# A group-norm attention block with five engines in one written order: bias load behind x, stores and divisions a burst later, last pair's q and k ahead of the output projection

## The chip, the cores and the metric

The kernel runs on one core of a Trainium2 chip. The metric is the device time of one execution in microseconds (us), the median of several executions. A core has five engines that matter here: TensorE (PE, matrix products), VectorE (DVE), ScalarE (ACT), GpSimd (POOL) and SyncE (SP), which here only issues DMA transfers. Each engine takes its own instructions in order and waits, where it must, on semaphores that the others and the DMA queues raise.

## The reference, cut to what matters

```python
x: (4, 512, 48, 48) float32            # batch, channels, 2304 pixels
hn  = group_norm(x, 32 groups)         # over 16 channels x 2304 pixels each
qkv = einsum('oc,bchw->bohw', qkv_w, hn) + qkv_b      # 1536 x 512, to float16
w   = softmax((q * s)^T (k * s))       # 8 heads of 64 channels, 2304 x 2304
a   = einsum('bhts,bhcs->bhct', w, v)  # float32 again
out = x + einsum('oc,bchw->bohw', proj_w, a) + proj_b
```

## The kernel before, in words

**Tiles.** A batch is four chunks of 128 channels by 2304 pixels, held in blocks of 512 pixels, the last of 256 (`QBLOCKS`, j = 0 to 4). Two heads make a pair; there are 16 pairs (`NG`), four to a batch. For a pair and a block of 512 query pixels the kernel goes over the 18 tiles of 128 key pixels. Three such tiles make a **burst**: six matmuls for the scores of both heads (line 871), three exponentials of 128x1024 on ScalarE (line 878), and two bursts later (`BEHIND`) six matmuls with v (line 896). The list `stream` holds all bursts, 27 to a pair and 432 in all; block j = 4 has bursts of twice as many matmuls of half the width. The row sums of the softmax are kept by VectorE, which adds each burst's exponentials into `acc` (line 929, two folds in line 932), and by a matmul with ones over the result (`add_up`, line 949).

**Filler.** All other matrix work is cut into pieces that stand in one list, `beside`: projections to q and k of later pairs (`pqk`, line 696), to v (`pv`, line 741), and the output projection of the batch before (`pr`, line 798). `fill(n)` runs once per burst n and issues as many pieces as a credit allows, in the order of the list; a piece may have an earliest burst and a condition. If the head of the list isn't allowed yet, the burst goes without filler. `do_tasks`, called at the start of `fill`, issues the small work of the next batch's normalisation: `bn_stats` (line 605), and 20 normalisations in place (line 647) on VectorE. The v projection of the next batch has a condition: its blocks must have been issued for normalisation.

**After a block of queries.** `values` copies the result out of PSUM (`avx`, line 905). `rows` in `add_up` copies the sums (`slx`, line 959) and sends them by DMA into a narrow tile (line 963). A burst later `check_sums` tests their range on POOL (lines 986 and 987) and `invert` takes the reciprocal and writes it to DRAM (lines 993 and 995). Another burst later `divide` loads it back, spread over 64 partitions per head (`ib`, line 1005), and multiplies on POOL (`att`, line 1008). `direct` blocks, the last two of the last pair, are divided on VectorE without the way through DRAM.

**Output projection.** `att32` casts four `att` tiles to a wide type (line 792, on POOL) into `a32`, of which there is one buffer; `proj_chain` makes eight matmuls per 128 output channels; `proj_end` adds bias and residual (line 809, VectorE) and stores at once (line 812). The residual is loaded two chunks ahead (line 770) into a tag `res` of three buffers, which the store must have left. `chain_bank` gives one PSUM bank (`pw`) to all filler.

**Start.** x of batch 0 and the weights are loaded, statistics are taken chunk by chunk of 128 channels, ScalarE normalises (line 654), and six q and k chains run over the chunks in an outer loop `for c`. Between the chains stand two small matmuls with `gmat` for the group mean (line 622, after chain i = 1) and the variance (line 631, after chain i = 3) of the next chunk. `gmat` is made on POOL by a memset and two selections (line 565). The bias of v reaches all partitions through a DRAM row `brow` and a broadcast `bv` (lines 522 and 526), both issued by POOL.

**Order.** The program is traced in one order. PE and DVE keep that order; the instructions of the other three engines are ordered by a scheduler:

```python
    with tc.manual_schedule(engines={mybir.EngineType.PE, mybir.EngineType.DVE}):
        fast_path(tc, flag, *args)
```

`general_path`, behind a test at the end, isn't run with this data.

Of the kernel before, what the change touches and what calls it, by code (L numbers as in the profile page):

```python
# [26 lines left out]
P = 128  # L27
# [440 lines left out]
def fast_path(  # L468
# [37 lines left out]
    def load_block(b, j):  # L506
# [13 lines left out]
    bv = const.tile([P, C], F32, name="bv")  # L520
    brow = dram.tile([1, C], F32, tag="brow", bufs=1, name="brow")
    nc.gpsimd.dma_start(
        brow.rearrange("a (n p) -> a n p", p=P),
        qkv_b[:, 2 * NC :].rearrange("p n -> n p").unsqueeze(0),
    )
    nc.gpsimd.dma_start(bv, brow.to_broadcast((P, C)))

# [14 lines left out]
    load_w(2, slice(0, C), nc.sync)  # L542

# [214 lines left out]

    atts, res, at32 = {}, {}, {}

    def residual(b, j, m):
        o, n = QBLOCKS[j]
        if at_end(b, j):

            tag = f"x{m}_{j - NQ + 2}"
            xt = xpool.tile([P, QB], F32, tag=tag, name=f"r_{b}_{j}_{m}")[:, :n]
        else:
            xt = work.tile([P, QB], F32, tag="res", bufs=3, name=f"r_{b}_{j}_{m}")
            xt = xt[:, :n]
        nc.sync.dma_start(xt, x[b, bass.ts(m, P), o : o + n])  # L770
        res[b, j, m] = xt
# [34 lines left out]
    def proj_end(b, j, m, ps):  # L806
        o, n = QBLOCKS[j]
        xt = res.pop((b, j, m))
        nc.vector.scalar_tensor_tensor(  # L809
            xt, ps[:, :n], bproj[:, m : m + 1], xt, ALU.add, ALU.add  # L810
        )
        nc.sync.dma_start(out[b, bass.ts(m, P), o : o + n], xt)

    def proj_pieces(b, j):


        n = QBLOCKS[j][1]

        def run(chunk):
            bank = chain_bank(f"pr_{b}_{j}_{chunk[0]}")  # L820
            places = [bank[:, i * n : (i + 1) * n] for i in range(len(chunk))]
            for m, ps in zip(chunk, places):
                proj_chain(b, j, m, ps)
            for m, ps in zip(chunk, places):
                proj_end(b, j, m, ps)

        def ahead(k):
            if k < NQ * NC and not at_end(b, k // NC):
                residual(b, k // NC, k % NC)

        convert = [
            piece(0.0, lambda: att32(b, j, (NC - 1,) if at_end(b, j) else range(NC)))
        ]
        chains = []
        per = QB // n
        for m in range(0, NC, per):
            chunk = range(m, m + per)
            loads = [j * NC + i + 2 for i in chunk]
            if (j, m) == (0, 0):
                loads = [0, 1] + loads  # L840
            chains.append(
                [piece(0.0, lambda i=i: ahead(i)) for i in loads]
                + [piece(QB / 290.0, lambda chunk=chunk: run(chunk), True, True)]
            )
        return convert, chains
# [3 lines left out]
    av, acc, pts, avx, sums, rowd = {}, {}, {}, {}, {}, {}  # L849
# [61 lines left out]
    def add(u):  # L911
# [6 lines left out]
        if last and direct(g, j):  # L918
            acc[g, j].append(pt)
            return  # L920
# [14 lines left out]
    def add_up(g, j):  # L935
# [31 lines left out]
        if direct(g, j):  # L967
            source = rows() if n == QB else sl
            inv = work.tile([P, QB], F32, tag="rows", name=f"inv_{g}_{j}")
            nc.vector.reciprocal(inv[:, :n], source[:, :n])  # L970
            nc.vector.tensor_tensor(
                atts[g][:, o : o + n], avx.pop((g, j))[:, :n], inv[:, :n], ALU.mult
            )
            if source is sl:
                rows()
        else:
            rows()
# [22 lines left out]
    def divide(g, j):  # L1000
        o, n = QBLOCKS[j]
        row = rowd.pop((g, j))
        ib = work.tile([P, QB], F32, tag="rows", name=f"ib_{g}_{j}")
        for h in range(2):
            nc.sync.dma_start(
                ib[h * D : (h + 1) * D, :n], row[h : h + 1, :n].to_broadcast((D, n))
            )
        nc.gpsimd.tensor_tensor(  # L1008
            atts[g][:, o : o + n], avx.pop((g, j))[:, :n], ib[:, :n], ALU.mult
# [13 lines left out]

    now = [0]
    tasks, loads = deque(), deque()
    normed, turn = set(), {}
# [24 lines left out]
    def group_scale(b):  # L1053
        group_rstd(b, norm_bank(b))
        tasks.append((now[0] + 1, lambda: coefficients(b)))
        for j in range(NQ):
            for c in range(NC):

                def run(j=j, c=c):
                    norm(b, j, c)  # L1060
                    normed.add((b, j, c))
# [16 lines left out]
    def put_v(b, half):  # L1078
        for i in range(0, NT, 2):
# [3 lines left out]
            if half == 0:  # L1083
                pieces[0][4] = lambda last=last: last in normed
# [5 lines left out]
    def ready(b, j):  # L1090

        return BEHIND + (2 if direct((b + 1) * NPAIR - 1, j) else 5)
# [11 lines left out]
    for b in range(B):  # L1104
# [13 lines left out]
        if b == B - 1:  # L1118
            put_convert(old, 0)
            put_qk(g + 3, 1)  # L1120
            for j in range(NQ):
                put_qk(g + 3, 0, (j,))
# [3 lines left out]
            for j in range(NQ - 2):  # L1126
                put_convert(b, j)
                put_proj(b, j)
                if j < 2:
                    for m in range(NC):  # L1130
                        put_run(residual, b, NQ - 2 + j, m)
# [59 lines left out]
    for c in range(NC):  # L1191
# [4 lines left out]
        for i, chain in enumerate(chains):  # L1196
            chain(c)
            if c + 1 < NC and i == 1:
                group_mean(0, small_bank(f"mean_0_{c + 1}"), (c + 1,))
            if c + 1 < NC and i == 3:  # L1200
# [16 lines left out]
    def fill(n):  # L1217
# [6 lines left out]
        do_tasks(5 if idle else 0 if ended(n - 1) else 1 if ended(n - BEHIND - 1) else 2)  # L1224
# [28 lines left out]
    for n in range(end):  # L1253
# [16 lines left out]
        if ended(n - BEHIND - 3):  # L1270
            divide(*stream[n - BEHIND - 3][:2])
# [8 lines left out]
    att32(B - 1, NQ - 1, (NC - 1,))  # L1280
    while beside:
        issue()
    check_sums(NG - 1, NQ - 1)
    for pieces in projs[B - 1, NQ - 1][1]:
        for p in pieces:
            p[1]()
# [10 lines left out]
def group_norm_attention(ctx: ExitStack, tc: tile.TileContext, *args):  # L1297
# [3 lines left out]
    with tc.manual_schedule(engines={mybir.EngineType.PE, mybir.EngineType.DVE}):  # L1301
# [46 lines left out]
```

## Time and profile before

| | |
|---|---|
| time, median of three runs | 1676.22 us (1675.67 to 1679.45) |
| span of the profiled execution | 1674.1 us |
| PE busy | 1597.4 us (95%) |
| DVE busy | 1131.2 us (68%) |
| ACT busy | 1246.4 us (74%) |
| POOL busy | 363.0 us (22%) |
| one exponential of 128x1024 (L878) | 1028 ns mean, 1296 of them |
| one add into `acc` (L929) | 1804 ns mean |
| one cast for the output projection (L792) | 904 ns mean |
| one division (L1008) | 1596 ns mean |
| one residual or output transfer of 256 KB | 2.8 and 2.4 us from issue to landing |

The page gives for each engine its busy time and share of the span; for groups of instructions their line, engine, operation, output and inputs, count, busy time, mean duration, and the idle time of the engine ahead of them with what ended it. "Issue" is idle time in which nothing in the profile was waited for. Windows can be asked for separately: each gives the busy time of every engine in a stretch of the span, the number of instructions, and the granted share of the TensorE clock (PEclk).

### The profile page before, as it was taken

What the parts mean: (1) busy time and instruction counts of PE and PEld (TensorE: products, weight loads), DVE (VectorE), ACT (ScalarE), POOL (GpSimd) and SP (SyncE); (2) the same over time, 40 slices, a digit from 0 to 9 for tenths busy, and PEclk for the clock granted to TensorE, in tenths of its full rate; (3) what the DMA queues carried; (4) which work ended last, traced back from release to release, by engine and by line L of the source; (5) the groups of instructions that cost most, each with busy time, mean ns of one, the idle gap of its engine ahead of it and who ended that gap; (6) DMA issues with size and microseconds to landing.
All of it is one profiled execution on the core that took longest, in us unless ns stands there. A gap on an engine that the chain in (4) does not pass through costs nothing.

```text
span 1674.1 us, 28357 instructions
## 1 busy us (share of the span) xinstructions
PE 1597.4 (95%) x11516; PEld 699.1 (42%) x11516; DVE 1131.2 (68%) x1284; ACT 1246.4 (74%) x1317; POOL 363.0 (22%) x500
## 2 busy tenths in 40 slices
PE   3999999989999999989999999999999999999897
PEld 1443344334333443545433344345533334444445
DVE  3247666887666667867666766787766666676774
ACT  2158788867887878867777878777777888877982
POOL 1002221211121111232112111233232122233431
PEclk9999999999999999999999999999999999999999
DMA  8001001300000003440200000353010000044232
GB/s 213 1 8 33 14 12 47 97 14 11 14 17 14 15 11 89 118 130 21 45 14 18 14 11 14 93 147 103 11 48 17 14 14 11 14 111 120 74 100 92
DMA packets 94908, 82.11 MB, mean 49 GB/s; under 512 B 50928, under 2 KB 61040, under 8 KB 94768
## 3 DMA queue, kind: packets, MB, share of 16 engines
q1 hardware_dynamic: 93168, 78.87, 17.7%
q8 instruction: 92, 1.51, 0.4%
q10 hardware_dynamic: 1344, 1.05, 0.2%
q0 software_dynamic: 256, 0.28, 0.1%
q14 instruction: 48, 0.39, 0.1%
HBM read 60.70 MB, written 19.17 MB: 48 GB/s over the span
## 4 chain that ended last, share of the span: by engine, by line
PE 89%; DVE 3%; ACT 3%; DMA 2%; POOL 1%; issue 1%; SPq 0%; POOLq 0%; DVEq 0%; ACTq 0%
PE pqk L696 29%; PE ps L871 18%; PE av L896 17%; PE pv L741 15%; PE pr L798 8%; ACT p L878 3%; PE sl L949 1%; PE ps L696 1%; DVE acc L929 1%; DMA brow<-qkv_b_dram 1%; POOL a L792 1%; DMA ib<-row 1%; DMA out_dram<-r 0%; DVE r L809 0%; POOL att L1008 0%
## 5 line engine op out<-in xcount | busy, mean ns | idle before, releaser
L878 ACT ACTIVATE p<-ps 128x1024 f16<-128x1024 f32 x1296 | 1231.5, 1028 | 363.3 <-PE ps L871 363.3
L929 DVE TENSOR_TENSOR acc<-acc,p 128x3072 f16<-128x3072 f16 x270 | 487.0, 1804 | 65.5 <-ACT p L878 65.2
L696 PE MATMUL pqk<-x,wqkv 128*64 128x512 f32 (+1 forms) x2464 | 518.2, 551 | 2.5 <-DVE r L809 1.7
L871 PE MATMUL ps<-q,k 64*128 64x512 f16 (+1 forms) x2880 | 363.9, 359 | 16.0 <-ACT p L878 14.7
L896 PE MATMUL av<-p,v 128*64 128x512 f16 (+1 forms) x2880 | 361.7, 365 | 0.0
L741 PE MATMUL pv<-wqkv,x 128*64 128x256 f32 x2304 | 269.4, 380 | 5.2 <-DVE x L647 5.0
L986 POOL TENSOR_SCALAR in<-sums 128x8 f32<-128x8 f32 (+1 forms) x160 | 111.5, 697 | 727.6 <-DMA sums<-slx 719.8
L696 PEld LDWEIGHTS pqk<-x,wqkv 128*64 128x64 f32 x2464 | 168.8, 137 | 229.1 <-issue 171.8
L871 PEld LDWEIGHTS <-k 64*128 64x128 f16 x2880 | 107.7, 94 | 296.5 <-issue 250.3
L896 PEld LDWEIGHTS <-v 128*64 128x64 f16 x2880 | 131.9, 109 | 210.5 <-issue 166.6
L1008 POOL TENSOR_TENSOR att<-avx,ib 128x512 f16<-128x512 f32 (+1 forms) x78 | 124.5, 1596 | 418.9 <-DMA ib<-row 381.0
L741 PEld LDWEIGHTS pv<-wqkv,x 128*64 128x64 f32 x2304 | 159.7, 137 | 99.7 <-DVE x L647 9.0
L929 DVE TENSOR_TENSOR acc<-p,p 128x3072 f16<-128x3072 f16 x80 | 141.4, 1768 | 0.3 <-ACT p L878 0.3
L798 PE MATMUL pr<-a,whi 128*128 128x512 f32 (+1 forms) x320 | 125.2, 399 | 8.9 <-POOL a L792 8.0
L798 PE MATMUL pr<-a,wlo 128*128 128x512 f32 (+1 forms) x320 | 117.4, 375 | 0.0
L705 DVE TENSOR_SCALAR q<-pqk,bqkv 128x512 f16<-128x512 f32 (+1 forms) x79 | 54.9, 695 | 89.9 <-PE pqk L696 89.5
L932 DVE TENSOR_TENSOR acc<-acc 128x1024 f16<-128x1024 f16 x156 | 110.8, 711 | 5.3
L749 DVE TENSOR_TENSOR v<-pv,bv 128x512 f16<-128x512 f32 x72 | 49.7, 691 | 92.7 <-PE pv L741 92.1
L705 DVE TENSOR_SCALAR k<-pqk,bqkv 128x512 f16<-128x512 f32 (+1 forms) x75 | 52.2, 696 | 78.1 <-PE pqk L696 77.8
L905 DVE COPY avx<-av 128x512 f32<-128x512 f32 (+1 forms) x80 | 51.0, 638 | 69.1 <-PE av L896 69.0
L809 DVE SCALAR_TENSOR_TENSOR r<-pr,bproj,r 128x512 f32<-128x512 f32 (+1 forms) x80 | 55.2, 695 | 62.2 <-PE pr L798 56.8
L792 POOL CAST a<-att 128x512 fp32r<-128x512 f16 (+1 forms) x78 | 68.1, 904 | 94.5 <-PE pr L798 93.7
(62 smaller groups left out, 457.5 us busy)
## 6 DMA issues: line engine op xcount, KB each, us to landing
r<-x_dram SPq DMA_DIRECT2D x64, 256.0 KB, 2.8
out_dram<-r SPq DMA_DIRECT2D x64, 256.0 KB, 2.4
ib<-row SPq DMA_DIRECT2D x126, 128.0 KB, 3.0
x<-x_dram SPq DMA_DIRECT2D x62, 256.0 KB, 3.1
x<-x_dram SPq DMA_DIRECT2D x16, 128.0 KB, 2.4
sums<-slx SPq DMA_DIRECT2D x128, 2.0 KB, 2.1
r<-x_dram SPq DMA_DIRECT2D x16, 128.0 KB, 2.2
out_dram<-r SPq DMA_DIRECT2D x16, 128.0 KB, 1.8
```

Of the source, the lines that this page charges most:

```text
L696: nc.tensor.matmul(pw[0][lo : lo + D, :n], wqkv[:, c, w0 + lo : w0 + lo + D], hn[b, c, j], start=(c == 0), stop=(c == NC - 1),)
L705: nc.vector.tensor_scalar(qk[g][part][:, o : o + n], pw[0][:, :n], bqkv[:, col : col + 1], SCALE, ALU.add, ALU.mult,)
L741: nc.tensor.matmul(pw[0][lo : lo + D, a, :], hn[b, c, i * P // QB][:, at + lo : at + lo + D], wqkv[:, c, 2 * C + half * C // 2 :][:, : C / ...
L792: engine.tensor_copy(at32[b, j][c], atts[b * NPAIR + c][:, o : o + n])
L798: nc.tensor.matmul(ps[:, :n], w[:, c, bass.ts(m, P)], at32[b, j][c], start=(c == 0 and i == 0), stop=(c == NC - 1 and i == 1),)
L871: nc.tensor.matmul(ps[:, h, a * n : (a + 1) * n], kt[rows, bass.ts(i, P)], qt[rows, o : o + n], start=True, stop=True,)
L878: nc.scalar.activation(pt[:, r], ps, AF.Exp)
L896: nc.tensor.matmul(av[0][lo : lo + D, :n], vv[b, pr // 2][:, i, pr % 2 * P + lo : pr % 2 * P + lo + D], pt[:, r, h, a * n : (a + 1) * n], ...
L929: nc.vector.tensor_tensor(t, before, pt, ALU.add)
L932: nc.vector.tensor_tensor(t[:, 0], t[:, 0], t[:, r], ALU.add)
L986: nc.gpsimd.tensor_scalar(t, sm, limit, None, op)
L1008: nc.gpsimd.tensor_tensor(atts[g][:, o : o + n], avx.pop((g, j))[:, :n], ib[:, :n], ALU.mult)
```

## The change

All five engines now follow the traced order, so POOL, SP and ACT wait exactly where the program puts their instructions. The author's purpose is to place loads, stores and divisions so that no queue stands still for something late. With it come these edits:

- **Bias load**: `brow` and `bv` go from POOL's queue, ahead of `gmat`, to SP's queue, behind x and the weights.
- **Start loop**: group mean after chain i = 0 instead of 1, variance after i = 2 instead of 3.
- **Stores and residuals**: a store is issued one burst after its addition; a residual is loaded one chunk ahead instead of two; the 256-wide blocks move two chunks by one transfer instead of two.
- **Divisions**: `divide` is split into `spread` (the loads of `ib`) and the multiplication one burst later, except in the last pair.
- **Normalisation**: `do_tasks` gets 2 or 4 tasks per burst where the filler stands still, instead of 5; a v piece waits until its blocks were normalised in an earlier burst.
- **Output projection**: conversion allowed six bursts after the sums instead of five; in the last batch q and k of the last pair come ahead of the output projection of batch 2, where they were mixed.
- **End**: the very last block sums three tiles by matmul instead of adding on VectorE first, and the second to last block's division moves from VectorE to POOL.

```diff
-    nc.gpsimd.dma_start(bv, brow.to_broadcast((P, C)))
...
     load_w(2, slice(0, C), nc.sync)
+    bv = const.tile([P, C], F32, name="bv")
+    brow = dram.tile([1, C], F32, tag="brow", bufs=1, name="brow")
+    nc.sync.dma_start(
+        brow.rearrange("a (n p) -> a n p", p=P),
+        qkv_b[:, 2 * NC :].rearrange("p n -> n p").unsqueeze(0),
+    )
+    nc.sync.dma_start(bv, brow.to_broadcast((P, C)))
...
-                proj_end(b, j, m, ps)
+            xt = res.pop((b, j, chunks[0]))
+            for i, m in enumerate(chunks):
+                nc.vector.scalar_tensor_tensor(
+                    xt[:, i], places[i], bproj[:, m : m + 1], xt[:, i], ALU.add, ALU.add
+                )
+            loads.append(
+                (now[0] + 1, lambda: nc.sync.dma_start(rows_of(out, b, j, chunks), xt))
+            )
...
-        if last and direct(g, j):
+        if direct(g, j) and (last or j == NQ - 1):
             acc[g, j].append(pt)
...
-            nc.vector.tensor_tensor(
+            engine = nc.vector if source is sl else nc.gpsimd
+            engine.tensor_tensor(
                 atts[g][:, o : o + n], avx.pop((g, j))[:, :n], inv[:, :n], ALU.mult
             )
...
-                pieces[0][4] = lambda last=last: last in normed
+                pieces[0][4] = lambda last=last: normed.get(last, now[0]) < now[0]
...
-        return BEHIND + (2 if direct((b + 1) * NPAIR - 1, j) else 5)
+        if b < B - 1:
+            return BEHIND + 6
+        return BEHIND + (2 if j >= NQ - 2 else 5)
...
         if b == B - 1:
+            put_qk(g + 3, 1)
+            put_qk(g + 3, 0)
             put_convert(old, 0)
-            put_qk(g + 3, 1)
             for j in range(NQ):
-                put_qk(g + 3, 0, (j,))
                 put_proj(old, j)
...
-            if c + 1 < NC and i == 1:
+            if c + 1 < NC and i == 0:
                 group_mean(0, small_bank(f"mean_0_{c + 1}"), (c + 1,))
-            if c + 1 < NC and i == 3:
+            if c + 1 < NC and i == 2:
                 group_rstd(0, small_bank(f"var_0_{c + 1}"), (c + 1,))
...
-        do_tasks(5 if idle else 0 if ended(n - 1) else 1 if ended(n - BEHIND - 1) else 2)
+        do_tasks(
+            (2 if idle else 0)
+            if ended(n - 1)
+            else (2 if idle else 1) if ended(n - BEHIND - 1) else 4 if idle else 2
+        )
...
-        if ended(n - BEHIND - 3):
-            divide(*stream[n - BEHIND - 3][:2])
+        if ended(n - BEHIND - 3) and not direct(*stream[n - BEHIND - 3][:2]):
+            spread(*stream[n - BEHIND - 3][:2])
+            if n >= end - per_pair:
+                divide(*stream[n - BEHIND - 3][:2])
+        if ended(n - BEHIND - 4) and stream[n - BEHIND - 4][:2] in ibs:
+            divide(*stream[n - BEHIND - 4][:2])
...
-    with tc.manual_schedule(engines={mybir.EngineType.PE, mybir.EngineType.DVE}):
+    kinds = mybir.EngineType
+    engines = {kinds.PE, kinds.DVE, kinds.Pool, kinds.SP, kinds.Activation}
+    with tc.manual_schedule(engines=engines):
```

## The prediction

> **What bounds the kernel now.** I read the page's busy times first (PE 1597.4 of 1674.1 us: the bound, with 76.7 us idle), then windows, to see where the idle lies. Columns: window, length, then busy us and count per engine, TensorE clock, DMA share, GB/s.
>
> ```profile
> 18.00:30.00 12.00, 5.75 (x16) 2.57 (x18) 7.43 (x22) 3.42 (x5) 1.39 (x3) 1.00 0.98 325
> 30.00:60.00 30.00, 24.70 (x118) 8.28 (x116) 11.09 (x36) 10.25 (x15) 1.66 (x3) 1.00 0.18 65
> 60.00:300.00 240.00, 238.78 (x1800) 103.61 (x1798) 144.27 (x150) 164.85 (x174) 37.90 (x47) 1.00 0.10 24
> 320.00:370.00 50.00, 40.76 (x310) 17.33 (x308) 41.84 (x65) 36.34 (x40) 12.20 (x16) 0.93 0.10 27
> 700.00:770.00 70.00, 63.04 (x396) 32.17 (x396) 48.74 (x70) 44.79 (x48) 17.75 (x28) 0.95 0.36 108
> 810.00:830.00 20.00, 18.33 (x118) 7.02 (x116) 12.74 (x14) 13.98 (x15) 4.83 (x9) 1.00 0.36 87
> 1090.00:1170.00 80.00, 76.04 (x482) 39.38 (x480) 64.42 (x85) 58.03 (x62) 30.43 (x33) 1.00 0.42 124
> 1560.00:1600.00 40.00, 30.16 (x209) 12.93 (x207) 28.59 (x29) 37.41 (x41) 17.12 (x20) 1.00 0.25 54
> ```
>
> PE idles 18 us before the first window, 6.3 and 5.3 in the first two, then 1.2, 9.2, 7.0, 1.7, 4.0 and 9.8 us; between them (370 to 700, 830 to 1090, 1170 to 1560) it is never idle, so nothing can be won there. The waits of PE name the causes:
>
> ```profile
> PE mean L622 <- POOL gmat L565: 18.9, 1, 18.9
> PE ps L871 <- ACT p L878: 14.7, 33, 0.5
> PE pr L798 <- POOL a L792: 8.0, 5, 4.9
> PE sl L949 <- DVE avx L905: 6.8, 4, 2.7
> PE pv L741 <- DVE x L647: 5.0, 5, 1.7
> ```
>
> The timeline of the start tells why gmat is late: its second selection stands on POOL behind bv, which waits for brow.
>
> ```profile
> 3.67 1.15 POOL L522 DMA_DIRECT2D brow<-qkv_b_dram  x1
> 9.13 0.29 DVE L610 BATCH_NORM_AGGREGATE mv<-st 128x2 f32<-128x30 f32 x1
> 17.89 0.57 POOL L526 DMA_DIRECT2D bv<-brow  x1 [12.27 <-DMA brow<-qkv_b_dram]
> 18.48 0.34 POOL L565 TENSOR_SCALAR_AFFINE_SELECT gmat<-gmat 128x128 f32<-128x128 f32 x1
> 24.55 3.42 ACT L654 ACTIVATE x<-x,gb,ga 128x512 f32<-128x512 f32 x5 [19.07 <-DVE gb L642]
> ```
>
> The largest single gap later is the pr wait of 4.9 us at 714: POOL's division waits for ib, and SP had sat on stores and residual loads.
>
> ```profile
> 713.77 0.47 SPq L1005 DMA_DIRECT2D ib<-row  x1
> 717.22 1.26 POOL L1008 TENSOR_TENSOR att<-avx,ib 128x512 f16<-128x512 f32 x1 [4.55 <-DMA ib<-row]
> 718.42 1.72 POOL L792 CAST a<-att 128x512 fp32r<-128x512 f16 x3
> ```
>
> **What the Trainium skill says.** "PSUM — Partial Sum Buffer", section "Engine vs sequencer instructions": the queues of ScalarE, VectorE and GpSimd are strict FIFO. The trace agrees: a selection of 0.34 us waits 12.27 us behind a DMA issue. "DMA: Bandwidth & Descriptors", section "Rules for kernel authors": a strided last dimension "lowers to one descriptor per element". brow is such a transfer; its 2 KB took 13.9 us, and in the first 30 us the DMA answer shows 390 GB/s at best but 14 to 27 GB/s between 12.75 and 16.5 us, while x was still outstanding. "TensorE: Matmul & The Clock Gate", section "What's actually happening": half clock after an idle window of about 3.4 us. The trace agrees: after the 4.9 us gap the granted clock was 0.80 in 710 to 720 and 0.86 in 720 to 730. "SBUF — State Buffer", section "Who interferes with whom": VectorE and GpSimd lock a shared port pair. Four casts took 2.39 us at 697 and 3.81 at 1123, which fits.
>
> **The change part by part.**
>
> *Start.* Without bv ahead, gmat ends near 6 us, and the first mean can start once mv is there, 9.13 + 0.29 = 9.4 us instead of 18.88: 9.4 us won. From mean to the first normalisation took 24.55 - 18.88 = 5.7 us, of which 2.8 are statistics of chunk 1, so these are wanted at 11.5 us. x and the first weights are 5.2 MB; at about 370 GB/s from 3 us on they land by 17 us, chunk 1 by 12, chunk 3 by 17 (wanted at 23): not in the way. The cycle of one chunk was 6.7 us (33.45, 40.19, 46.92), 0.87 of it PE waiting for ScalarE, since the variance stood after chain 3; one chain earlier is 0.97 us earlier, which closes it, three times: 2.6 us. Sum 12.0. bv is needed by the first v at about 59 us; issued near 17 us it has 40 us for the 14 and 6 us that brow and bv took: free. Bounds 9 to 13.
>
> *First change of batch (320 to 370).* The compiled order has nine bursts without filler instead of six, since v waits a burst longer and normalisations come slower. VectorE bounds here. From the add of a block's last burst at 328.74 to the sums of the next block at 360.3 before took 31.6 us, with 7.5 us of v work inside (64 matmuls, 16 per 1.89 us), so 24.1 without. The new order of the same stretch on VectorE is six adds of 1.74, four folds of 0.76, 8 statistics (5.1 in all with the aggregates), 2 avx and 2 slx of 0.69, 5 normalisations of 0.63 and 1.5 us of small ones: about 26. So 1.9 us worse, plus up to 2 of its own waits; 1.5 us of waiting for x, which came after (361), goes. I take 2 worse, bounds 4 worse to 2 better.
>
> *Second (700 to 830).* Idle 7.0 + 1.7, and about 1.9 us of half clock under busy PE: 10.5. With ib issued a burst (3.6 us) before the multiplication and stores that SP no longer waits long for (the DMAs take 2.4 to 3.0 us), the 4.9 and 1.7 go. What stays: a32 has one buffer, so each of four changes of block may cost 0.7, as a gap at 1110 shows (casts 0.95 us each against 0.47 us of matmuls): 2.8. New: one burst without filler. Such a burst costs 0.84 (ten of them at 1560 to 1600 waited 8.4 us for ScalarE). With 0.5 for VectorE: 4.1, so 6.4 won, bounds 4 to 8.5.
>
> *Third (1090 to 1170).* Idle 4.0; after: the same 2.8 and one new burst without filler: 0.3 won.
>
> *Last batch.* Before, bursts 406 and 408 to 417 have no filler, eleven, and 9.8 us of idle. After, burst 408 and 415 to 417: four, 3.4 us. But pr of batch 2 is now in one run, where qk pieces gave POOL time: three changes of block of 0.7, and 0.6 for the sums: 6.1. Won 3.8, bounds 1.5 to 5.5. Divisions in the last pair wait for ib on POOL, but 8 us or more pass before their casts are needed.
>
> *Tail.* PE waited 2.71 us at 1646.8 for avx behind division (0.69) and add (1.75) on VectorE:
>
> ```profile
> 1646.08 0.69 DVE L971 TENSOR_TENSOR att<-avx,inv 128x512 f16<-128x512 f32 x1
> 1646.69 1.75 DVE L929 TENSOR_TENSOR acc<-p,p 128x3072 f16<-128x3072 f16 x1
> ```
>
> Both leave; twelve more ones matmuls (0.65 us for twelve) come: 1.6 won. Merged 256-wide transfers are off the path.
>
> Sum: 12.0 - 2.0 + 6.4 + 0.3 + 3.8 + 1.6 = 22.1 us, 1676.2 - 22.1 = 1654.1.
>
> **Waits added.** Every ib load now sits on SP behind a store that waits for VectorE's addition of the burst before; POOL's casts stand behind a multiplication that waits for ib. Both are a burst old when met, against 3 us of DMA: no wait in a burst of 3.6 us, a short one in a burst of 2.75.
>
> **Rivals.** (1) Start and tail only: DVE stalls and added bursts without filler (5 new ones, 7 gone) eat the middle: 1676.2 - 13.6 = 1662.6. For it: VectorE has 41.8 of 50 us in the first change. Against: the two POOL stalls are queue order, which is what changes. (2) More than forecast: casts hide (there was no gap over 0.3 us at the changes of block at 697 and 733), VectorE catches up: 2.8 + 2 + 3 more, 1646. (3) Slower: in strict order POOL or SP blocks for something the scheduler used to step around. One stall as at 714 costs 4.9 + 1.9 = 6.8 us; four such beyond those removed, with no gain in the middle: 1662.6 + 27 = 1690. Against: only x reloads, which wait for PE, and stores could do it, and neither stands before work that is due within a burst.
>
> **How the numbers follow.** Forecast 0.62, rival 1 0.23, rival 2 0.10, rival 3 0.05. The range reaches from rival 2 to past rival 1: 1645 to 1666. All but rival 3 are faster by over 0.2% (3.4 us); a tie would need half of rival 3's stalls: 0.02.
>
> **What would show it.** Mean L622 starting near 9.4 us and no bv on POOL; normalisation cycle near 5.9 us; PE idle about 11 us in the first change of batch; no pr wait over 2 us, and no half clock at the second; waits of pr for a summing to 8 us; ps for p about 13; sl for avx at the end under 1 us. Wrong would be: DVE or POOL waits over 3 us new in PE's list, x landing later than 20 us, or v waiting for bv.

## The result, and the profile after

The kernel after takes 1661.52 us (median, 1660.74 to 1665.11); the kernel before took 1676.01 us beside it. The ratio is 0.9913, 95% interval 0.9894 to 0.9932: 14.5 us less. The forecast was 22.1 us less (1654.1 us); the result is inside the range, and where the first rival put it (1662.6 us). Of the profiled executions the span fell from 1674.1 to 1659.0 us, and all of it is idle time of TensorE: PE is busy for 1597.6 us (1597.4 before) and idle for 61.4 us (76.7 before).

The windows of the kernel after, laid round the same stages as before (columns: window, length, busy us and count of PE, PEld, DVE, ACT, POOL, then TensorE clock, DMA share, GB/s):

```profile
0.00:15.50 15.50, 1.14 (x4) 1.00 (x4) 8.19 (x22) 2.02 (x3) 4.28 (x16) 1.00 0.94 304
15.50:60.00 44.50, 41.65 (x206) 15.59 (x208) 15.77 (x45) 12.94 (x20) 1.67 (x3) 1.00 0.32 96
310.00:350.00 40.00, 30.68 (x222) 12.37 (x222) 36.51 (x54) 33.66 (x37) 10.16 (x11) 0.96 0.22 54
670.00:760.00 90.00, 84.04 (x546) 44.15 (x542) 70.24 (x94) 63.35 (x68) 26.43 (x38) 0.98 0.43 125
1080.00:1160.00 80.00, 73.69 (x476) 38.69 (x474) 63.31 (x83) 54.98 (x59) 28.08 (x36) 1.00 0.40 119
1490.00:1560.00 70.00, 64.73 (x405) 32.59 (x402) 46.91 (x47) 51.37 (x55) 27.58 (x33) 1.00 0.41 120
1560.00:1600.00 40.00, 36.17 (x227) 17.78 (x226) 28.96 (x30) 33.21 (x36) 14.45 (x19) 1.00 0.43 130
1600.00:1659.00 59.00, 46.33 (x324) 30.13 (x321) 29.55 (x37) 23.77 (x26) 15.29 (x28) 0.95 0.37 123
```

Length less PE busy is the idle of each stage:

| stage | idle before, us | idle after, us | won | forecast |
|---|---|---|---|---|
| start, 0 to 60 | 29.5 | 17.2 | 12.3 | 12.0 |
| first change of batch | 9.2 | 9.3 | -0.1 | -2.0 |
| second change | 8.6 | 6.0 | 2.7 | 6.4 (with half clock) |
| third change | 4.0 | 6.3 | -2.4 | 0.3 |
| last batch, to 1600 | 9.8 | 9.1 | 0.7 | 3.8 |
| tail | 14.1 | 12.7 | 1.5 | 1.6 |

The start and the tail are as forecast. The middle, forecast at 8.5 us, brought 0.9 us of idle. Half clock adds a little: outside its last microseconds the kernel before has TensorE busy for 9.1 us at half clock and the kernel after for 6.1 us, so 1.5 us less are lost, 1.1 of them at the first change and 0.4 at the second. With it the first change came 1.0 us better and the second 3.1 us.

The waits of PE in the kernel after (what waited, for whom: us in total, times, longest):

```profile
PE ps L892 <- ACT p L899: 14.9, 33, 0.5
PE pr L819 <- POOL a L813: 10.8, 13, 1.5
PE mean L622 <- DVE mv L610: 9.1, 1, 9.1
PE sl L970 <- DVE avx L926: 4.7, 3, 2.1
PE pr L819 <- DVE r L839: 3.3, 3, 2.7
```

The wait for `gmat` is gone (the first mean now waits for `mv`), and so is the single wait of 4.9 us for a cast. In its place stand thirteen waits for casts, 10.8 us in all where there were five with 8.0, and a new one of 2.7 us for the residual addition `r`.

The start is as the steps had it. Its timeline (start us, length, engine, line, operation; in brackets the idle before it and its releaser):

```profile
4.00 0.76 POOL L565 TENSOR_SCALAR_AFFINE_SELECT gmat<-gmat 128x128 f32<-128x128 f32 x2
9.11 0.55 PE L622 MATMUL mean<-mv,gmat 128*128 128x1 f32 x2 [9.11 <-DVE mv L610]
14.76 3.42 ACT L654 ACTIVATE x<-x,gb,ga 128x512 f32<-128x512 f32 x5 [9.42 <-DVE gb L642]
32.31 0.35 SPq L542 DMA_DIRECT2D bv<-brow  x1
```

`gmat` ends at 4.8 us, the first mean starts at 9.1 us (9.4 forecast), the first normalisation at 14.8 us (24.6 before), and the later ones follow 5.9 us apart (23.67, 29.54, 35.42), as forecast. `bv` is issued at 32 us, lands at 38.2 us, and v first needs it at 60.1 us. x profits too: its last block lands at 17.8 us, where it landed at 27.2 us before. `brow`, a transfer of 2 KB, is no faster at its new place (15.4 to 32 us, and from 25 us on next to nothing else moves), but now nothing that is due stands behind it.

The new wait at the second change (the same columns):

```profile
674.62 1.05 SPq L791 DMA_DIRECT2D r<-x_dram  x2
676.07 2.98 SPq L503 DMA_DIRECT2D x<-x_dram  x4
680.50 0.75 DVE L839 SCALAR_TENSOR_TENSOR r<-pr,bproj,r 128x512 f32<-128x512 f32 x1 [4.32 <-DMA r<-x_dram]
681.31 0.80 PE L819 MATMUL pr<-a,whi 128*128 128x512 f32 x1 [2.69 <-DVE r L839]
```

The first residual is issued 2.5 us before its addition could start (the matmuls end at 677.1 us), and behind four x reloads, issued from 670.2 us on, that only land between 676 and 679 us. It lands 6 us after its issue; the addition waits, and PE behind it, since all filler has one PSUM bank. The matmul after the gap takes 0.80 us where the same one takes 0.50 elsewhere: half clock.

The kind of wait that is new at the third change:

```profile
1094.46 1.27 POOL L1034 TENSOR_TENSOR att<-avx,ib 128x512 f16<-128x512 f32 x1 [7.49 <-DVE st L605]
1095.68 4.73 POOL L813 CAST a<-att 128x512 fp32r<-128x512 f16 x4
1097.87 0.50 PE L819 MATMUL pr<-a,whi 128*128 128x512 f32 x1 [1.51 <-POOL a L813]
```

Four casts of an older block stand in GpSimd's queue behind a division of a newer one, and that waits for its `ib`, which SyncE issued at 1090.6 us after it had stood at a residual load that needed a store's buffer. (The row names a statistics instruction of VectorE that has nothing to do with `att`; the transfer of `ib`, which landed at 1094.3 us, is what the division needs. What `ib` is loaded from had itself landed only at 1089.7 us, so the stand at the residual cost 0.9 us at most.)

### The profile page after: what moved, and what is told of

Read it like the earlier page. It is cut to its first block, busy times and chain, and to the rows that moved or that the text cites. A ratio compares the mean times of both kernels' runs of the same rounds, so it can differ in the third digit from the quotient of the medians.

```text
span 1659.0 us, 28335 instructions
## 1 busy us (share of the span) xinstructions
PE 1597.6 (96%) x11528; PEld 699.7 (42%) x11528; DVE 1131.3 (68%) x1282; ACT 1246.5 (75%) x1317; POOL 370.8 (22%) x499
## 3 DMA queue, kind: packets, MB, share of 16 engines
q10 hardware_dynamic: 1344, 1.05, 0.2%
## 4 chain that ended last, share of the span: by engine, by line
PE 87%; DVE 4%; DMA 3%; POOL 3%; ACT 2%; issue 1%; SPq 0%; ACTq 0%; DVEq 0%; POOLq 0%
PE pqk L696 28%; PE ps L892 17%; PE av L917 17%; PE pv L741 15%; PE pr L819 7%; POOL a L813 2%; ACT p L899 2%; DVE acc L950 2%; PE ps L696 1%; PE sl L970 1%; DMA row<-inv 1%; DVE acc L953 1%; DMA ib<-row 1%; DMA out_dram<-r 1%; DVE st L605 0%
## 5 line engine op out<-in xcount | busy, mean ns | idle before, releaser
L892 PE MATMUL ps<-q,k 64*128 64x512 f16 (+1 forms) x2880 | 362.3, 358 | 17.0 <-ACT p L899 14.9
L1034 POOL TENSOR_TENSOR att<-avx,ib 128x512 f16<-128x512 f32 (+1 forms) x78 | 132.8, 1703 | 447.0 <-DMA ib<-row 366.1
L819 PE MATMUL pr<-a,whi 128*128 128x512 f32 (+1 forms) x320 | 126.5, 403 | 14.0 <-POOL a L813 10.8
L839 DVE SCALAR_TENSOR_TENSOR r<-pr,bproj,r 128x512 f32<-128x512 f32 (+1 forms) x80 | 54.7, 693 | 63.4 <-PE pr L819 56.2
L819 PEld LDWEIGHTS pr<-a,whi 128*128 128x128 f32 x320 | 60.5, 189 | 56.5 <-POOL a L813 22.6
```

What stands on the lines that cost most here:

```text
L819: nc.tensor.matmul(ps[:, :n], w[:, c, bass.ts(m, P)], at32[b, j][c], start=(c == 0 and i == 0), stop=(c == NC - 1 and i == 1),)
L839: nc.vector.scalar_tensor_tensor(xt[:, i], places[i], bproj[:, m : m + 1], xt[:, i], ALU.add, ALU.add)
L892: nc.tensor.matmul(ps[:, h, a * n : (a + 1) * n], kt[rows, bass.ts(i, P)], qt[rows, o : o + n], start=True, stop=True,)
L1034: nc.gpsimd.tensor_tensor(atts[g][:, o : o + n], avx.pop((g, j))[:, :n], ibs.pop((g, j))[:, :n], ALU.mult,)
```

## The experiments

All times are medians, each set against runs of the kernel before on the same chip; "won" is the difference of the two medians. The ratio is estimated from all runs, so it can differ from that of the medians by a microsecond or so. The intervals are about 0.2% (3.3 us) to each side, so two variants that differ by less than some 5 us aren't told apart by their times. What tells them apart is PE's idle, stage by stage. The last column but one is the length of the stretches at half clock, without the one that every profile has at its end, when PE has finished.

| | time, us | won, us | ratio, 95% interval | PE idle, us | half clock, us | pr waits for casts, us |
|---|---|---|---|---|---|---|
| before | 1676.01 | | | 76.7 | 13.7 | 8.0 |
| after | 1661.52 | 14.5 | 0.9913, 0.9894 to 0.9932 | 61.4 | 6.8 | 10.8 |
| e1 start only | 1665.81 | 11.9 | 0.9922, 0.9902 to 0.9942 | 65.5 | 13.7 | 8.8 |
| e2 cast tiles | 1660.19 | 17.5 | 0.9895, 0.9877 to 0.9914 | 58.4 | 17.1 | 6.4 |
| e3 residual early | 1664.09 | 13.6 | 0.9909, 0.9889 to 0.9929 | 61.7 | 17.1 | 11.6 |
| e4 q, k mixed again | 1669.64 | 8.0 | 0.9941, 0.9918 to 0.9964 | 63.2 | 20.5 | 6.2 |
| e5 division last | 1659.16 | 18.9 | 0.9890, 0.9871 to 0.9910 | 59.1 | 13.7 | 6.3 |
| e6 residual one ahead | 1668.16 | 9.9 | 0.9938, 0.9914 to 0.9961 | 63.4 | 20.5 | 9.8 |
| e7 scheduler orders | 1658.71 | 19.4 | 0.9879, 0.9858 to 0.9900 | 59.3 | 17.1 | 10.5 |
| e8 old pace | 1665.81 | 12.3 | 0.9933, 0.9911 to 0.9955 | 61.2 | 13.6 | 10.4 |
| e9 three mends | 1652.96 | 24.4 | 0.9860, 0.9843 to 0.9876 | 55.5 | 6.8 | 2.0 |
| e10 mends, scheduler | 1653.02 | 24.3 | 0.9864, 0.9847 to 0.9882 | 55.1 | 10.2 | 6.3 |
| e11 old mean places | 1669.46 | 7.9 | 0.9957, 0.9940 to 0.9973 | 66.9 | 20.5 | 10.6 |
| e12 e9, scheduler | 1653.90 | 22.8 | 0.9860, 0.9838 to 0.9881 | 54.8 | 13.6 | 5.8 |

A stretch at half clock costs half of the time that PE is busy in it; where PE idles anyway it costs nothing. Idle plus that half explains the spans to within 4 us: taken off, 1591 to 1595 us are left in every one of the fourteen profiles (1674.1 - 76.7 - 4.6 = 1592.8 before, 1659.0 - 61.4 - 3.0 = 1594.6 after, 1649.7 - 55.5 - 3.4 = 1590.8 in e9).

**e1: the start alone, on the kernel before.**

```diff
-    nc.gpsimd.dma_start(bv, brow.to_broadcast((P, C)))
...
     load_w(2, slice(0, C), nc.sync)
...
+    nc.sync.dma_start(bv, brow.to_broadcast((P, C)))
...
-            if c + 1 < NC and i == 1:
+            if c + 1 < NC and i == 0:
...
-            if c + 1 < NC and i == 3:
+            if c + 1 < NC and i == 2:
```

> The kernel before with nothing but the two edits of the start: brow and bv on SyncE's queue behind x and the weights, group mean and variance one chain earlier. My theory (the two waits of the start are the whole of its gain, and they are independent of everything later): 12 us less than before, 1664 us, with PE idle of about 17 us in the first 60 us instead of 29.5 and nothing changed after 60 us. Then the rest of the change brings only 2 to 3 us. Rival (the start's lead is eaten at the first change of batch, because a later normalisation is what waits): 6 us or less, 1670 us or more.

Measured: 11.9 us won, idle in the first 60 us 17.6 us (29.5 before), and later stages as before, with a cast wait of 5.7 us at the second change. My theory holds: nothing eats the start's lead. So all the rest of the change is worth about the 4 us by which the idle differs (65.5 against 61.4); by the times it is 1.5 us (ratios) to 2.6 us (medians), which the intervals don't tell from nothing.

**e11: the mean and variance back at their old places, in the kernel after.**

```diff
-            if c + 1 < NC and i == 0:
+            if c + 1 < NC and i == 1:
...
-            if c + 1 < NC and i == 2:
+            if c + 1 < NC and i == 3:
```

> The kernel after with the group mean and variance of the start back at their old places (after chains 1 and 3 instead of 0 and 2). As I forecast (2.6 us, 0.87 us of TensorE waiting for ScalarE in each of three cycles of a chunk): the cycle goes from 5.9 to 6.7 us, TensorE idle in the first 60 us from 17.2 to 19.8 us, time 2.6 us more, 1664 us, so that the bias load alone is worth 9.4 us of the 12. Rival (with x only just arriving the cycle is bound by statistics or by x, not by the variance): 1 us or less.

Measured: the normalisations stand 6.7 us apart again (23.98, 30.72, 37.46), with three gaps of 0.87 us, and PE idles 20.1 us in the first 60 instead of 17.2: 2.9 us, against 2.6 forecast. The time won is 6.6 us less than that of after, which the start alone does not explain; in the profile the rest lies later, 6.1 us more lost at half clock and 2.5 us of idle, most of it behind gaps from 680 us on that this edit does not make. So of the start's 12.3 us of idle some 9.4 are the bias load's and 2.9 the loop's. By the first exponential (99.6 us before, 90.1 in e11, 88.1 after) it is 9.5 and 2.0 us.

**e2: four cast tiles instead of one.** The space stays the same; only what a cast has to wait for gets smaller.

```diff
-                t = work.tile([P, NC, QB], F32R, tag="a32", bufs=1, name=f"a32_{b}_{j}")
-                at32[b, j] = [t[:, c, :n] for c in range(NC)]
+                at32[b, j] = [
+                    work.tile([P, QB], F32R, tag=f"a32_{c}", bufs=1, name=f"a32_{b}_{j}_{c}")[:, :n]
+                    for c in range(NC)
+                ]
```

> The kernel after, with the target of the casts (a32) as four tiles of one chunk each, instead of one tile of four: a cast may start when the last matmuls on its own quarter are done, up to 6 matmuls or 1.4 us earlier. Theory (the single buffer is what PE waits for at each change of block): the waits of pr for a fall from 10.8 us to 2 us or less and the time falls by 8 to 10 us, 1652 us. Rival 1 (GpSimd's rate limits, four casts of 0.95 us against 0.47 us of matmuls each): 3 to 5 us, 1657 us. Rival 2 (the casts hide another wait of the same length, for VectorE or ScalarE): less than 2 us, the wait turning up under another name.

In e2 the row of PE's waits for casts is

```profile
PE pr L821 <- POOL a L815: 6.4, 8, 2.1
```

Measured: the waits for casts fall from 10.8 to 6.4 us and the idle by 3 us. That is the size of rival 1, but not its cause. In the kernel after, the gaps at 724, 1114, 1131, 1517 and 1532 us (0.7 to 1.3 us, 5.4 in all) had casts released by the last `pr` matmul of the block before; these gaps are gone. Those at 1096, 1499 and 1602 us (2.1, 1.4 and 1.4 with their small followers) stay, and in each the cast comes straight behind a division. So there are two causes, of about equal size, where I had named one.

**e5: the division behind the filler of its burst.**

```diff
-            if n >= end - per_pair:
-                divide(*stream[n - BEHIND - 3][:2])
-        if ended(n - BEHIND - 4) and stream[n - BEHIND - 4][:2] in ibs:
-            divide(*stream[n - BEHIND - 4][:2])
         if not summed:
             fill(n)
+        if ended(n - BEHIND - 3) and n >= end - per_pair:
+            if stream[n - BEHIND - 3][:2] in ibs:
+                divide(*stream[n - BEHIND - 3][:2])
+        if ended(n - BEHIND - 4) and stream[n - BEHIND - 4][:2] in ibs:
+            divide(*stream[n - BEHIND - 4][:2])
```

> The kernel after, with each burst's division issued behind its filler, so that on GpSimd a conversion of the same burst (four casts) stands ahead of the division and no longer behind it. Theory (at 1096, 1497 and 1602 us the casts were late because the division ahead of them waited for ib; 4.9 of the 10.8 us of pr waits): these three groups of gaps go, waits of pr for a fall to 5.9 us, time 1657 us. Rival (the casts wait for their single buffer or for att itself in these places too): waits of pr for a stay at 9 us or more, time unchanged within 1 us.

In e5 the same row, and GpSimd's order ahead of 1500 us, where in the kernel after a division of 1495.86 us stands ahead of the casts:

```profile
PE pr L819 <- POOL a L813: 6.3, 9, 1.3
1491.91 3.87 POOL L813 CAST a<-att 128x512 fp32r<-128x512 f16 x4
1498.17 1.27 POOL L1034 TENSOR_TENSOR att<-avx,ib 128x512 f16<-128x512 f32 x1 [2.40 <-DVE acc L950]
```

Measured: the groups at 1499 and 1602 us go, that at 1096 shrinks to a wait of 0.7 and 0.3 us for the buffer, and 6.3 us of cast waits are left against 5.9 expected. The idle falls only by 2.3 us, because waits for `r` rose by 1.1 us (3.2 us in one, at 680) and other small ones with them. At 1602 us the four casts that are due still start behind the division, at 1599.1 us; what moved ahead of it, from 1599 to 1591 us, are three casts for a later block that had stood between. So in these places GpSimd's order holds the casts back: the trace gives it, and a change of order takes it away, all of it at two places and half of it at 1096 us, where the buffer would have cost 1.0 us anyway.

**e3: the first two residuals of a batch ahead of the last x reloads.**

```diff
-                [piece(0.0, lambda k=k: ahead(k)) for k in ([0] if k == 0 else [])]
-                + [piece(0.0, lambda k=k: ahead(k + 1))]
+                [piece(0.0, lambda k=k: ahead(k + 1)) for k in range(k, k + 1) if k > 0]
...
+            if j == 2 and b > 0:
+                for jj, chunks in proj_list[:2]:
+                    put([piece(0.0, lambda old=old, jj=jj, chunks=chunks: residual(old, jj, chunks))])
             if j == 3 and b > 0:
                 put_convert(old, 0)
```

> The kernel after, with the first two residual loads of each batch issued ahead of the q and k pieces of block j = 2 of that stretch (in the last batch ahead of the conversion), so ahead of the last x reloads, instead of just before their matmuls. Theory (the new wait of 2.7 us at 678, and the half clock of 3.4 us after it, come from a 256 KB residual load that was issued behind eight x loads that saturate the DMA): the wait and the half clock go, 2.7 + 1.7 = 4.4 us, 1657 us. Rival (the DMA is the bound in that stretch, so the load that goes first delays the others, and v or statistics wait for x instead): less than 1 us.

Measured: the wait at 678 us and the half clock behind it are gone; between bursts 92 and 180 the idle falls from 3.5 to 0.9 us and the stretch from 318.8 to 314.9 us, 3.9 of the 4.4 us expected. Yet the whole did not get faster: stretches at half clock, 3.4 us each, now follow gaps at 1094, 1498 and 1605 us, where the kernel after has gaps of 1.5, 0.9 and 1.4 us without one. That the wait comes from a residual issued too late is shown; a gain in the time is not, from this run. Why the transfer then took 6 us was only read from the trace: in e3 the two residuals are issued at 642 us, 32 us earlier, ahead of those reloads, and each lands within 3.4 us. In the kernel after, four x reloads (not the eight of the expectation, of which four come later) and two `ib` loads stood ahead of it, took 5.4 to 7.0 us themselves, and the DMA share was 1.00 from 676 to 678 us and 1.05 from 678 to 680 us.

**e6: the residual really one chunk ahead.** `ahead` is a piece without cost, so it runs at the end of the burst before, behind the very store whose buffer it needs. Here it runs inside the next piece.

```diff
-        def run(chunks):
+        def run(chunks, k):
+            if k > 0:
+                ahead(k + 1)
...
-                [piece(0.0, lambda k=k: ahead(k)) for k in ([0] if k == 0 else [])]
-                + [piece(0.0, lambda k=k: ahead(k + 1))]
-                + [piece(QB / 290.0, lambda chunks=chunks: run(chunks), True, True)]
+                [piece(0.0, lambda k=k: ahead(k)) for k in ([0, 1] if k == 0 else [])]
+                + [piece(QB / 290.0, lambda k=k, chunks=chunks: run(chunks, k), True, True)]
```

> The kernel after, with the residual load of chunk k + 1 issued inside the piece of chunk k, behind the store of chunk k - 1, instead of as a piece of its own that runs at the end of the burst before (there it stands behind the store that it needs, and SyncE stood 110 us in 44 waits of 2.5 us for stores). Theory (these waits hold the ib loads behind them, and so the divisions and casts): SyncE's waits for stores fall from 110 us to under 30 us, ib is issued up to 3 us earlier, the groups of gaps at 1096 and 1497 us (2.1 and 1.4 us) shrink by half or more, time 1659 us. Rival (ib is late for the time of its own DMA chain, or the residual now comes too late for its addition): waits of pr for a stay near 10.8 us and waits for r rise over 3.3 us, time 1661 to 1665 us.

The rows of SyncE's waits that answer it, in the kernel after:

```profile
SPq L791 <- DMA out_dram<-r: 110.4, 44, 4.7
```

and in e6:

```profile
SPq L791 <- DMA out_dram<-r: 4.5, 8, 1.2
```

SyncE's waits for stores went as expected, but the casts' waits stayed at 9.8 us and those for `r` rose to 3.8 us: the rival. SyncE then waits for the additions themselves (71 us instead of 39, before the stores). In the tail, a residual now issued just before its addition made a cast of the last block and PE wait 2.9 us at 1645 us. The group at 1096 us shrank from 2.1 to 1.3 us, those at 1499 and 1602 us stayed or grew (1.4 and 1.8 us). So SyncE's long waits are real and were, but for some 0.8 us, not what PE paid for.

**e4: q and k of the last pair mixed again.**

```diff
-            put_qk(g + 3, 1)
-            put_qk(g + 3, 0)
             put_convert(old, 0)
+            put_qk(g + 3, 1)
             for j in range(NQ):
+                put_qk(g + 3, 0, (j,))
                 put_proj(old, j)
```

> The kernel after, with the last pair's q and k pieces mixed with the output projection of batch 2 again, as in the kernel before; bursts without filler rise from 19 to 26. As I forecast (3.8 us won by this edit): 3.8 us slower, 1665 us. By the idle of the two profiles (0.7 us won, because seven bursts without filler at 0.84 us were paid with waits for casts): 0.5 to 1 us slower, 1662 us, with the pr waits for a lower by 3 us or more.

Measured: idle 1.8 us more in all, and 2.2 us more from burst 396 on; waits of `ps` for exponentials rise from 14.9 to 18.3 us and waits for casts fall from 10.8 to 6.2 us. The time won is 6.5 us less; of the 9.0 us by which the profiled span is longer, 6.9 were lost at half clock. By the idle the edit is worth 2 us, between the two expectations: it saves 3.4 us of waits for exponentials and 1.6 for `avx`, and pays 4.6 back in casts; the rest is in small waits.

**e8: the old pace of normalisation.**

```diff
-        do_tasks(
-            (2 if idle else 0)
-            if ended(n - 1)
-            else (2 if idle else 1) if ended(n - BEHIND - 1) else 4 if idle else 2
-        )
+        do_tasks(5 if idle else 0 if ended(n - 1) else 1 if ended(n - BEHIND - 1) else 2)
-                pieces[0][4] = lambda last=last: normed.get(last, now[0]) < now[0]
+                pieces[0][4] = lambda last=last: last in normed
```

> The kernel after, with the old pace of normalisation (five tasks in a burst where the filler stands still, none or one at the end of a block) and the old condition on v (block issued for normalisation in the same burst). Bursts without filler fall from 19 to 14 (71 to 73, 183, 294 and 408 go, 400 comes). As I forecast (the new pace costs 2 us at the first change, by five instead of three... three more bursts without filler there, and one each later): 4 us of waits of ps for p go, waits of pv for x of 4 to 5 us come, 1660 us. Rival (the bursts without filler were the real price, and the waits of v for x hide behind what VectorE has to do anyway): 1657 us. Other rival (the new pace is a gain, as its waits are shorter): 1663 us or more.

Measured: `ps` waits 4.8 us less for exponentials, `pv` waits 4.3 us for x again, and the idle is the same, in all (61.2 against 61.4 us) and at the first change (9.4 against 9.3). Of the three times only the last, 1663 us or more, lies in its interval (7.5 to 14.9 us won), but e8 isn't told apart from after either, and it lost 3.8 us more at half clock. By the idle the new pace exchanges one wait for another of the same length.

**e7: the scheduler orders GpSimd, SyncE and ScalarE again, all other edits kept.**

```diff
-    engines = {kinds.PE, kinds.DVE, kinds.Pool, kinds.SP, kinds.Activation}
+    engines = {kinds.PE, kinds.DVE}
```

> The kernel after, but with GpSimd, SyncE and ScalarE ordered by the scheduler again, as in the kernel before; TensorE's, VectorE's and ScalarE's instructions stand in exactly the same order as after, only GpSimd's and SyncE's move. As I forecast (the written order is what removes the stall of 4.9 us at the second change of batch): a stall of 4 us or more at the second change comes back, 1666 us or more. Rival (the scheduler steps around what is late, and the written order costs as much in casts behind divisions as it saves): within 2 us of after, 1660 to 1664 us.

Measured: each is right in one half. The stall at the second change is back, with 6.8 us of half clock behind it. The timeline of e7 there:

```profile
722.74 1.26 POOL L1034 TENSOR_TENSOR att<-avx,ib 128x512 f16<-128x512 f32 x1 [4.47 <-DMA ib<-row]
723.95 2.29 POOL L813 CAST a<-att 128x512 fp32r<-128x512 f16 x4
```

PE waited 4.2 us for this cast. But the late residual and the casts behind divisions at 1096, 1497 and 1602 us are gone (one of 1.2 us came at 1547), and the kernel is not slower for it: 19.4 us won against 14.5, with intervals that overlap a little. So the written order of GpSimd and SyncE, the headline of the change, brought no time here; it exchanged stalls of 4.2 and 1.2 us for others that together are no shorter (2.7 us for the residual and up to 4.9 us for casts).

**e9: e2, e3 and e5 together, in the written order.**

> The kernel after with three edits together: the cast target in four tiles (as in e2), the division behind the filler (as in e5), and the first two residual loads of each batch ahead of the last x reloads (as in e3). Theory (the waits are separate: buffer 5.9 us, casts behind a division 4.9 us, first residual 2.7 us and half clock behind these gaps 3 to 5 us): waits of pr for a and for r together fall from 14.1 us to under 3 us, TensorE idle from 61 to about 51 us, time 1649 us, below both kernels. Rival (they hide each other: where one goes, the next ends at nearly the same time): time no less than 1655 us.

The waits of PE in e9 that answer the expectation:

```profile
PE pr L821 <- DVE r L841: 3.1, 5, 1.2
PE pr L821 <- POOL a L815: 2.0, 4, 0.8
```

Casts and residuals together cost 5.1 us instead of 14.1. The idle falls by 5.9 us rather than 10, as waits of `ps` for VectorE's small group-norm instructions (`veps` and `gmean`, 5.1 us together, 1.8 in the kernel after) come up. The time is 1652.96 us, between theory and rival, and its interval lies below that of after: this version beats both kernels.

**e10: the scheduler's order with the tiles and the early residuals; e12: e9's edits with the scheduler's order.**

> The kernel after with the scheduler ordering GpSimd, SyncE and ScalarE again (as in e7), the cast target in four tiles and the early first residuals, and without the edit of the division's place. Theory (with the scheduler what is left is one stall of 4.2 us behind a division at the second change of batch and 6.3 us of waits for the buffer; only the second goes): 1653 us, some 4 us over e9. Rival (the scheduler, given room by the tiles, places the casts ahead of the division by itself): within 1 us of e9 or below it.

> The kernel of e9 (cast target in four tiles, division behind the filler, first residuals early), with GpSimd, SyncE and ScalarE ordered by the scheduler as in e10. Theory (the scheduler's order costs nothing by itself; what e10 still lost were two groups of casts behind a division, 2.5 and 2.9 us, and these go with the program's order of the two): waits of pr for a under 2 us, TensorE idle 51 us, 1649 us, 4 us below e9. Rival (the scheduler puts a division ahead of casts by its own estimate, whatever the program's order): as e10, 1653 us.

Measured: 1653.02 and 1653.90 us, neither told apart from e9. e10 came at the time that I expected, but not 4 us above e9. In e12 the rival holds: the scheduler still puts a division ahead of casts, and the waits at 722 and 1540 us (2.5 and 2.9 us in e10) are 2.4 and 2.5 us. So once the casts have their own tiles and the residuals are early, the written order and the scheduler's come to the same time.

## Why the prediction was right in the start and too high in the middle

**Start, 12.0 forecast.** Right in the mechanism and in the size: 12.3 us of idle, split by e11 into 9.4 and 2.9. Of it 0.7 us are lost again in the first q and k chains, whose `ps` matmuls take 24.4 us in all instead of 23.7; at the first exponential the lead is 11.5 us. One reading was off, without effect: the best DMA rate in the first 30 us of the kernel before is 410 GB/s, not 390.

**First change, 2.0 worse.** It came out equal in idle. The step that failed is the sum of VectorE's work against bursts without filler: I charged the added bursts and credited only 1.5 us of the `pv` waits for x that the same edit removes. Before, these were 1.7, 0.8 and 1.5 us in this stage, and all three are gone; e8, over the whole kernel, has 4.3 us of them for 4.8 us of `ps` waits.

**Second change, 6.4 won.** The stall of 4.9 us went and e7 brings it back: the mechanism was right. 2.7 us of idle came and 0.4 us of half clock (PE lost 1.9 us to it before and 1.5 after, where none was forecast), 3.1 in all. The step that failed is "stores that SP no longer waits long for", and with it the sentence on x reloads and stores that "neither stands before work that is due within a burst": I looked at stores and took residual loads as harmless at one chunk ahead, though the timeline of before has x reloads at that place. The first residual of the batch has 2.5 us, and it took 6 us behind them.

**Third change, 0.3 won.** It got 2.4 us worse. Two terms were mis-sized. A change of block costs 1.3 us about as often as 0.7: I took 0.7 from the gap at 1110 us, while the trace of before also has one of 1.33 us at 1126. And "both are a burst old when met, against 3 us of DMA" failed: the division of 1094.5 us starts only as its `ib` lands, 3.8 us after it was first issued, and the casts behind it pay. GpSimd's idle time ahead of divisions is not new by itself (366 us in the kernel after, 381 before); that casts which are due stand behind it is. "PSUM — Partial Sum Buffer", section "Engine vs sequencer instructions", of the Trainium skill, which I had cited for bv and gmat (strict FIFO queues), is what I failed to apply to the cast behind the division; the trace agrees (the cast at 1095.7 us starts as the division ends, and e5 undoes it).

**Last batch, 3.8 won.** 0.7 in the stage, 2 by e4. The same two terms: casts at 1499, 1517, 1532, 1552 and 1602 us wait 0.9, 0.7, 1.3, 0.5 and 1.4 us, where I had charged three of 0.7. The remark that divisions of the last pair have "8 us or more" before their casts looked at their own casts alone; at 1602 us it is an older block's that stand behind one.

**Tail, 1.6 won.** 1.5, by the profile; no run takes the tail's edits alone, nor the later stores or the merged transfers. The wait of `sl` for `avx` went from 2.71 to 0.52 us.

**Rivals.** Rival 1 named the result, start and tail only, but for the wrong reason: not VectorE stalls and bursts without filler, but casts and the residual; that it hit the number is luck. Rival 2's claim that casts hide is refuted in the kernel after, and e9 shows what it takes to make it nearly true (2.0 us of waits left). Rival 3's mechanism, a strict order that blocks, is what happened, in small: 2.7 us once and up to 4.9 us in three places, not four stalls of 6.8. That the residual was issued too late was shown by e3; that the x transfers ahead of it are what slowed it, and that the time of `ib`'s own DMA chain makes the divisions late, was only read from the traces.

## What to carry to other kernels

A queue that is written by hand should have, at each place, the instruction whose consumer is due first, and the one that waits for a long DMA chain last; here casts behind a division, at three places together, cost up to 4.9 us, as much as the stall that the new order removed. A scheduler's order may do as well: e10 and e12 are as fast as e9. Where a buffer is the limit, splitting its tile can be enough: in e2 it took away gaps of 5.4 us at no space. And when a change is said to be about order, try the start and every other edit apart from it: here 9.4 of the 15.3 us of idle that went came from one bias load that had stood ahead of an instruction of 0.3 us.

## What the runs showed of the hardware

In all fourteen profiles the stretches at half clock start on a fixed grid of 3.413 us within a profile, and last one or two of its steps. Cutting the time from 60 to 1640 us of each profile along that grid gives 6481 windows; 45 had PE busy for less than half, and 42 of these were followed by a window at half clock; of 32 between 0.5 and 0.6 nine were; of the other 6404, eight. So a gap of 1.5 to 2.1 us may cost nothing or 1.7 us more, as it falls into one window or across two: the gap at 1600 us is 1.77 us in e2, leaves its window 54% busy, and no half clock follows; at 1605 us in e3 it is 1.80 us, leaves its window 47% busy, and one does. "TensorE: Matmul & The Clock Gate", section "What's actually happening", of the Trainium skill has the free-running window of that length, and half clock after an idle one; the runs agree on the length, but a window that was busy for less than half was enough, also in the kernel before, where the two windows that the gap of 4.9 us lies in are 45% and 11% busy and neither is idle whole. This is why kernels here that differ by 1 to 3 us of idle can't be ranked by their times: before the end, half clock made up 6.8 to 20.5 us, 3.0 to 10.0 us of lost time, and where a stretch falls depends on the grid as well as on the edit.
